# Computing the value rows of two contexts inside the router's closing steps, and moving key rotations and a root in the attention prelude

## The chip, the cores and the metric

The kernel is one program on one core of a Trainium2 chip. The metric is the device time of one execution in microseconds (us). A kernel's time is the median of several executions. A profile is one more execution, recorded by the hardware profiler; its times are counted from the start of its span.

The engines have short names in the profile: PE is TensorE (matrix multiplies), PEld is its load of the stationary operand, DVE is VectorE, ACT is ScalarE, POOL is GpSimd, and SP is the engine whose queue issues most of the transfers (SPq). Each engine works through its own instructions in order and waits on semaphores for the others.

## What is computed

The reference is a two-layer decoder in float32 with a layer norm after each residual:

```
x   [4, 512, 256]      ctx [4, 1601, 256]      out [4, 512, 256]
x = LN(x + ttt(x))                              # one inner gradient step per token
x = LN(x + softmax(q k^T / 16 + side) ctx)      # cross-attention, additive side mask [512, 1601]
x = LN(x + moe(x))                              # 8 experts of width 1024, the best 2 per token
x = LN(x + causal_self_attention(x, 16 heads))
x = LN(x + cross_attention(x, ctx, 16 heads))   # rotary positions on q and k, padding mask
x = LN(x + ffn(x))                              # integer weights, scaled back
```

Two parts matter here. The first is the router of the experts: `softmax(x Wr + br)`, the two best experts of each token, and for each token its rank among the tokens that chose the same expert, which is the row that it is copied to. The second is the input of the last cross-attention, which depends on the four contexts alone: keys `rope(ctx Wk + bk)` and values `ctx Wv`, for 1601 positions and 16 heads of 16 columns. The rotation multiplies by a cosine, the neighbour-swapped copy by a sine, and adds the two. The values do not depend on anything that the first layer computes.

## The kernel before

The kernel is one long function. Its stages, by the profile's clock, are:

- 0 to about 270 us: the first layer's inner-step part.
- To about 520: the first cross-attention and the router (pool `p2`, line 605 on). A loop goes over 4 contexts x 4 query tiles of 128 rows. Each step scores a tile against 1601 positions, transposes the exponentials, and multiplies them with the context (`weighted`). The contexts stand in SBUF transposed (`ctxTs[b]`) and in rows (`ctxa`, `ctxb`); the side mask is the tile `fs`.
- 523 to 1023: the experts, 23 blocks of 256 rows (8 fixed and 15 chosen at run time).
- 1024 to 1078: the prelude of the second layer's attention.
- To about 1480: self-attention, 16 units (4 sequences x 4 groups of four heads).
- To 2313: cross-attention, 16 more units, numbered 16 to 31.
- To 2438: the feed-forward part.

**The router's closing steps.** After the fourth query tile of a context, `closing(b)` is queued. It is a generator, and each call of `tail()` runs it to its next `yield`: statistics and the root of the variance; the four tiles normalised (line 726); nothing; the transposes of `to_xT` (lines 188 and 196); nothing; the logits of `route`; softmax; the first choice; the second choice; the counts (lines 485 to 497); the matmul of the ranks, `bank<-both,before`; and the target rows. For the first three contexts these steps are interleaved with the next context's work. For the last one nothing is left to interleave, so they run one behind the other. Then `scatter(3)` copies the rows of x to the buffer `xs` by eight indirect transfers on POOL (line 534), and `blocks_left()` works out which blocks the experts have to run. The PSUM buffers of `bank()` rotate over two.

The order of the instructions on every engine in this stage is the program's order (`tc.manual_schedule()`) up to `ordered.close()`; the few steps behind it are placed by a scheduler.

**The prelude.** `context(b, keys, values, here)` returns work items. A key item is a matmul, an eviction with bias by ACT into a tile `raw` (four buffers, shared with the rows of self-attention), a neighbour swap on DVE and three elementwise steps (`rotated`, lines 1149 to 1152), and a transfer of the result to DRAM (`kcd`) that SP issues one key item later. A value item is two matmuls of 128 positions and an ACT copy into `vals[b % 2]` (line 1191). Context 0's keys (`keys0`, eight items: two halves of four chunks, 512, 512, 512 and 65 positions wide) and the values of contexts 0 and 1 are done here. Beside them, `combined(0)` gathers the experts' outputs for sequence 0 and adds them (`add` holds the sums, the statistics, the root and the normalisation, lines 125 to 171), and `turn` transposes the result. `first_sums` does the same sums for sequence 1 on POOL, in four rounds (lines 1075, 1099 and 1100). `k0_` and `q0_` (line 1124) make the first rows of self-attention, which go through DRAM (`ksd`, `qd`) and come back regrouped by head.

**The units.** Each unit loops over tiles k of 128 keys. A step takes scores (line 1310), exponentials (line 1324) and the weighted sum of the step before (line 1337), and at the same time the next unit's scores are taken once more for their maxima (lines 202, 1267 and 1269). A list of work items per unit (`extras`) is spread over its steps. A step without an item does the weighted sum in two halves of 256 queries. A step with an item does it in one, followed by the item. In the kernel before, the keys and values of contexts 2 and 3 are such items, of the units 16 to 27:

```
later = [
    context(2, range(4), ()) + context(3, range(2), ()),
    context(3, range(2, 4), ()) + context(2, (), range(4)),
    context(3, (), range(4)),
]
```

Their source, `cx`, is loaded from the transposed context in chunks, two ahead. Unit 20 + n, for n from 0 to 7, holds 1, 4, 4, 4, 4, 3, 3 and 3 value items, 26 in all.

Of the kernel before, what the change touches and what calls it, by code (L numbers as in the profile page):

```python
# [9 lines left out]
F32 = mybir.dt.float32  # L10
# [7 lines left out]
P = 128  # L18
B, S, D = 4, 512, 256
S2 = 1601  # L20
NT = S // P
NKT = (S2 + P - 1) // P
# [3 lines left out]
NH, HD = 16, 16  # L26
# [8 lines left out]
def kn_of(kt):  # L35
    return P if kt < NKT - 1 else KLAST
# [3 lines left out]
def decoder(ctx: ExitStack, tc: tile.TileContext, a: dict, out: bass.AP):  # L40
    nc = tc.nc
# [16 lines left out]
    def bank():  # L58
        return psum["B"].tile([P, 512], F32, tag="bank", name="bank")
# [15 lines left out]
    def weight(pool, name):  # L75

        src = a[name]
        t = pool.tile([P, 2, src.shape[1]], F32, tag=name, name=name)
        nc.sync.dma_start(t, src.rearrange("(c p) n -> p c n", p=P))
        return t  # L80
# [117 lines left out]
    def mm(ps, terms):  # L198

        n = len(terms)  # L200
        for i, (l, r) in enumerate(terms):
            nc.tensor.matmul(ps, l, r, start=(i == 0), stop=(i == n - 1))  # L202
# [3 lines left out]
    p2in = ph2in.enter_context(tc.tile_pool(name="p2in", bufs=1))  # L206


    with (
# [15 lines left out]
        ps = wide()  # L225
# [4 lines left out]
        ps = bank()  # L230
# [7 lines left out]
        fs = p2in.tile([P, NT, S2], F32, tag="fs", name="fs")  # L238
# [7 lines left out]
        KHALF = (NKT + 1) // 2  # L246
# [121 lines left out]
        going, waiting, turn = [ttt(0)], [1, 2, 3], 0  # L368
# [236 lines left out]
        return wrow, xrow  # L605


    with tc.tile_pool(name="p2", bufs=2) as p2, ExitStack() as ordered:


# [5 lines left out]
        ps = wide()  # L616
# [3 lines left out]
        ps = bank()  # L620
# [3 lines left out]
        ps = wide()  # L624
# [3 lines left out]
        ps = bank()  # L628
# [7 lines left out]
        ctxTs, ctxns = {0: ctx_first[0]}, {0: ctx_first[1]}  # L636
# [105 lines left out]
        scored(*steps[0])  # L742
        tails = []

        def tail():
            if tails and next(tails[0], tails) is tails:
                tails.pop(0)

        for i in range(len(steps) + 1):
            if i + 1 < len(steps):  # L750
                b, t = steps[i + 1]
# [9 lines left out]
            if i > 0:  # L761
                b, t = steps[i - 1]
# [3 lines left out]
                        ctxns[b + 1] = load_ctx(b + 1)  # L766
                    tails.append(closing(b))
            tail()
        while tails:
            tail()  # L770
        ordered.close()
        scatter(B - 1, lambda inst: unordered("xs", inst))
        wrow, xrow = blocks_left()
    ph2in.close()


# [2 lines left out]


    QS = 1.0 / math.sqrt(HD)
    VW = HD + 1
    p4a = late_a.enter_context(tc.tile_pool(name="p4a", bufs=1))
    mrow = tc.dram_tile((4 * B, S2), F32, name="mrow")
    live = p4a.tile([P, 4 * B], F32, tag="live", name="live")
# [35 lines left out]
    with tc.tile_pool(name="p3", bufs=2) as p3, ExitStack() as ordered:  # L821
# [180 lines left out]
        n = E + NDYN  # L1002
# [23 lines left out]
    with ExitStack() as s4:  # L1026
# [17 lines left out]
        def one():  # L1044
            return spare() if alone else ps1.tile([P, 512], F32, tag="one", name="one")

        diagq, later_, qt, kself, ngs, vself, vals = (
            ready[k] for k in ("diagq", "later", "qt", "ks", "ngs", "vself", "vals")
        )
# [10 lines left out]
        index = {u: i for i, u in enumerate(units)}  # L1060
        extras = [[] for _ in range(len(units) + 3)]
        quiet = [[] for _ in range(len(units) + 3)]
        starts = [[] for _ in range(len(units) + 3)]
# [109 lines left out]
        def context(b, keys, values, here=None):  # L1173


            def key(src, i, c, eng):
                flush(1)
                k0, kw = chunks[i]
                ps = one()
                mm(ps[:, :kw], [(W["xaK"][:, h, c * P : (c + 1) * P], src()[h][:, :kw]) for h in range(2)])  # L1180
                raw = raw_tile()
                nc.scalar.activation(raw[:, :kw], ps[:, :kw], AF.Identity, bias=bkc[:, c : c + 1])  # L1182
                rotated(raw, kw, slice(k0, k0 + kw), eng, ready["turn", i] if here else None)
                going.append(lambda: to_rows(kcd[b], c, k0, kw, raw[:, :kw]))

            def value(src, k):
                kn, c0 = kn_of(k), (k % 4) * P
                ps = one()[:, :D]
                mm(ps[:kn], [(src()[c][:, c0 : c0 + kn], W["xaV"][:, c, :]) for c in range(2)])
                dst = vals[b % 2][:kn, k, : NH * VW].rearrange("p (h r) -> p h r", r=VW)  # L1190
                nc.scalar.copy(dst[:, :, :HD], ps[:kn].rearrange("p (h r) -> p h r", r=HD))

            items = []
            for i in sorted({*keys, *values}):
                if here is None:
                    src = lambda n=len(stream): chunk(n)
                    stream.append((b, i))
                else:
                    src = lambda i=i: here[2 * i : 2 * i + 2]
                eng = nc.gpsimd if here is None else nc.vector  # L1200
                if i in keys:
                    items += [lambda s=src, i=i, c=c: key(s, i, c, eng) for c in range(2)]
                if i in values:
                    items += [lambda s=src, k=k: value(s, k) for k in range(4 * i, min(4 * i + 4, NKT))]
            return items
# [339 lines left out]
        ends1, n = {}, 0  # L1545
# [55 lines left out]
        keys0 = context(0, range(4), (), here=qt + kself)  # L1601
        (k0_, q0_), rows0 = self_rows(0, 0)
        (k1_, q1_), rows1 = self_rows(0, 1)
        for f in keys0[0:2] + values1 + add + keys0[4:6] + turn:
            f()
        for f in (k0_, q0_, rows0, *self_values(0), *keys0[2:4], *keys0[6:8]):
            f()
# [2 lines left out]
        flush(0)  # L1610
        for i, (n0, n1) in enumerate(((0, 4), (4, 6), (6, 7), (7, 8))):
            extras[i] = ([k1_, q1_, rows1] if i == 0 else []) + keys1[n0:n1] + extras[i]
        later = [
            context(2, range(4), ()) + context(3, range(2), ()),
            context(3, range(2, 4), ()) + context(2, (), range(4)),
            context(3, (), range(4)),
        ]
        for b, work in enumerate(later):
            for g in range(NG):
                n = -(-len(work) // (NG - g))  # L1620
# [233 lines left out]
```

## Time and profile before

| | |
|---|---|
| median of 3 executions | 2437.68 us (2436.15 to 2438.79) |
| profiled execution | 2439.88 us |
| its span | 2438.0 us, 1.88 less |
| TensorE busy | 2344.4 us of the span (96%) |
| VectorE, ScalarE, GpSimd busy | 1211.7, 1073.5 and 422.7 us |
| TensorE busy in the stage 1480 to 2313 | 832.48 of 833 us |
| TensorE busy in the prelude, 1024 to 1078 | 47.40 of 54 us |

The page gives the busy time of each engine, then the span in 40 slices of 61 us, where the row PEclk is the clock that TensorE was granted, in tenths of full speed. The chain that ended last follows the last instruction back to whatever released it. A line of the timeline has the start, the duration (of a run of like instructions, if it ends in x2 or more), the engine, the source line, the operation with its tiles, the shapes, and in brackets how long the engine had been idle and what ended that. A line of the windows has the window and its length, then for each engine its busy time and its count of instructions, then the granted clock, the share of the transfer engines' time and the rate in GB/s.

### The profile page before, as it was taken

The page shows a single profiled execution, that of the slowest core. Times are in us where ns is not written, and L with a number is a line of the kernel's source. Part 1 is how long each engine was busy: PE and PEld are TensorE (multiplying, and loading weights), DVE is VectorE, ACT ScalarE, POOL GpSimd, SP SyncE. Part 2 cuts the span into 40 slices and gives each one's busy share as a digit, 9 for nine tenths or more (in the row PEclk, how much of TensorE's full clock was granted, in tenths as well). Part 3 has the DMA queues.
Part 4 walks back from the last instruction along what each step waited for, and adds up shares of the span by engine and source line. Part 5 has one row for each costly group of instructions (what it writes and reads, how often), then busy time and mean ns, then how long its engine had stood idle before and what let it go on. Part 6 is the DMA issues. An engine that isn't in the chain of part 4 may idle for free.

```text
span 2438.0 us, 34867 instructions
## 1 busy us (share of the span) xinstructions
PE 2344.4 (96%) x13928; PEld 1328.2 (54%) x13928; DVE 1211.7 (50%) x2854; ACT 1073.5 (44%) x1996; POOL 422.7 (17%) x429
## 2 busy tenths in 40 slices
PE   7898999959999999989999999999999999999998
PEld 4767677748888888843333334333333333333256
DVE  1333334322222233266656667666666666677334
ACT  1111122114444544424555453655666566566730
POOL 1010001121144433345130010222110010000000
PEclk9999999969999999989999997999999999999999
DMA  8300311145667555351211210112110110100100
GB/s 307 150 1 3 124 54 45 49 143 186 247 239 266 198 204 201 124 164 50 66 48 35 95 36 5 39 51 60 51 37 16 45 36 16 30 34 18 31 9 26
DMA packets 76112, 215.84 MB, mean 89 GB/s; under 512 B 11816, under 2 KB 35630, under 8 KB 66862
## 3 DMA queue, kind: packets, MB, share of 16 engines
q1 hardware_dynamic: 61790, 133.04, 16.1%
q0 software_dynamic: 10992, 65.54, 7.3%
q10 hardware_dynamic: 3168, 15.03, 1.8%
q8 instruction: 110, 1.80, 0.3%
q14 instruction: 52, 0.43, 0.1%
HBM read 171.53 MB, written 53.21 MB: 92 GB/s over the span
## 4 chain that ended last, share of the span: by engine, by line
PE 51%; ACT 1%; DVE 1%; issue 0%; DVEq 0%; ACTq 0%
PE s L1310 23%; PE one L202 12%; PE po L1337 11%; PE s L202 2%; PE s L1320 1%; PE one L1295 1%; PE one L1358 1%; ACT x L171 0%; ACT ex L1324 0%; DVE one L1269 0%; PE one L1379 0%; PE one L1477 0%; PE one L1400 0%; DVE pm L1267 0%; DVE st L156 0%
## 5 line engine op out<-in xcount | busy, mean ns | idle before, releaser
L1324 ACT ACTIVATE ex<-s 128x512 f32<-128x512 f32 (+1 forms) x1062 | 577.9, 594 | 466.9 <-PE s L1310 236.7
L1267 DVE TENSOR_REDUCE pm<-one 128x1 f32<-128x512 f32 x768 | 493.7, 685 | 174.5 <-PE s L1310 123.3
L1310 PE MATMUL s<-q,kc 32*128 32x512 f32 x1612 | 524.1, 640 | 0.2 <-ACT ex L1324 0.2
L202 PE MATMUL one<-kc,qt 32*128 32x512 f32 (+1 forms) x2048 | 483.8, 564 | 0.3 <-DVE pm L1267 0.3
L1310 PEld LDWEIGHTS s<-q,kc 32*128 32x128 f32 x1612 | 161.6, 179 | 210.9 <-issue 175.5
L1337 PE MATMUL po<-ex,v 128*32 128x256 f32 (+3 forms) x2472 | 245.1, 465 | 0.3 <-ACT ot L1350 0.3
L1269 DVE CUSTOM_DVE_ANT_0 one<-one,c_diagq 128x512 f32<-128x512 f32 x256 | 171.9, 716 | 75.6 <-PE one L202 63.5
L1310 PE MATMUL s<-q,ks 32*128 32x512 f32 x512 | 179.8, 650 | 5.3 <-ACT ex L1324 4.9
L1337 PEld LDWEIGHTS po<-ex,v 128*32 128x32 f32 (+1 forms) x2472 | 49.8, 108 | 232.2 <-issue 225.5
L886 DVE TENSOR_TENSOR g<-g,sg 128x1024 f32<-128x1024 f32 x46 | 57.2, 1243 | 235.8 <-ACT sg L883 235.7
L202 PE MATMUL wide<-xbT,eWi 128*128 128x256 f32 x736 | 168.9, 389 | 4.0 <-DVE xbT L858 4.0
L202 PEld LDWEIGHTS one<-kc,qt 32*128 32x128 f32 x2048 | 164.2, 188 | 11.6 <-DVE pm L1267 7.9
L202 PE MATMUL wide<-xbT,eWg 128*128 128x256 f32 x736 | 162.6, 379 | 0.0
L202 PE MATMUL bank<-eWo,g 128*128 128x256 f32 x736 | 162.5, 379 | 0.0
L202 PEld LDWEIGHTS wide<-xbT,eWi 128*128 128x128 f32 x736 | 143.5, 196 | 25.8 <-issue 4.2
L202 PE MATMUL one<-ks,qt 32*128 32x512 f32 x512 | 152.6, 665 | 3.7 <-ACT raw L1182 2.7
L202 PEld LDWEIGHTS wide<-xbT,eWg 128*128 128x128 f32 x736 | 139.7, 190 | 19.2 <-ACT g L883 0.2
L1150 POOL TENSOR_TENSOR raw<-raw,c_cos 128x512 f32<-128x512 f32 (+1 forms) x32 | 34.9, 1092 | 660.5 <-DVE swp L1149 578.1
L202 PEld LDWEIGHTS bank<-eWo,g 128*128 128x128 f32 x736 | 138.2, 190 | 17.9
L883 ACT ACTIVATE g<-wide,eWi 128x256 f32<-128x256 f32 x184 | 71.7, 476 | 72.3 <-PE wide L202 69.7
L1310 PEld LDWEIGHTS s<-q,ks 32*128 32x128 f32 x512 | 53.8, 185 | 83.4 <-issue 62.0
L202 PE MATMUL wide<-ctxT,q 128*128 128x512 f32 (+1 forms) x256 | 91.3, 510 | 0.8 <-DVE q L649 0.8
(319 smaller groups left out, 2988.4 us busy)
## 6 DMA issues: line engine op xcount, KB each, us to landing
xs<-zero SPq DMA_DIRECT2D x32, 512.0 KB
kc<-kcd SPq DMA_DIRECT2D x16, 800.5 KB
eWo<-in_eWo SPq DMA_DIRECT2D x8, 1408.0 KB
cx<-in_ctxT SPq DMA_DIRECT2D x18, 512.0 KB
eWi<-in_eWi SPq DMA_DIRECT2D x8, 1028.0 KB
eWg<-in_eWg SPq DMA_DIRECT2D x8, 1028.0 KB
qt<-qd SPq DMA_DIRECT2D x32, 256.0 KB
ctxT<-in_ctxT SPq DMA_DIRECT2D x4, 1601.0 KB
```

The costliest lines, as they stand in the source:

```text
L202: nc.tensor.matmul(ps, l, r, start=(i == 0), stop=(i == n - 1))
L883: nc.scalar.activation(dst[:, k, :], pv[:, k, :], func, bias=bias)
L886: nc.vector.tensor_tensor(part, part, dst, ALU.mult)
L1150: eng.tensor_tensor(raw[:, :n], raw[:, :n], cos[:, :n], ALU.mult)
L1267: nc.vector.tensor_reduce(pm[:, t, j, c : c + 1], ps, AX.X, ALU.max)
L1269: nc.vector.tensor_tensor_reduce(out=ps, in0=ps, in1=diagq[:, 384 - t * P : 896 - t * P], scale=1.0, scalar=LOWEST, op0=ALU.add, op1=ALU.m ...
L1295: nc.tensor.transpose(pt[:, t * P : (t + 1) * P], ng.rearrange("p j r -> p (j r)"), ident)
L1310: nc.tensor.matmul(ps[:kn], kt[rows, k * P : k * P + kn], q2[rows, :], start=True, stop=cross)
L1320: nc.tensor.matmul(ps[:, k * P : (k + 1) * P], later_[:, :P], later_[:, P:], start=False, stop=True)
L1324: nc.scalar.activation(ex[:kn, h, :], ps[:kn], AF.Exp)
L1337: nc.tensor.matmul(state["po"][j * 32 : j * 32 + 32, q0:q1], (vals if cross else vself)[b % 2][:kn, k, c0 : c0 + 32], ex[:kn, j % 2, q0:q1 ...
L1358: nc.tensor.transpose(pt[:, t * P : (t + 1) * P], ot[:, t * P : (t + 1) * P], ident)
```

## The change

The change has four parts.

1. The values of contexts 2 and 3 are computed in the router stage, from the contexts that stand there. They go into two tiles that take over the memory of the side mask and of half of the last context's rows. DVE sets the ones and zeros around them (six memsets, placed behind the second closing step). The 26 value steps stand between the closing steps of the last context: four ahead of the transposes, twelve ahead of the rank matmul, ten behind `blocks_left()`, which now comes before `ordered.close()` and `scatter(3)`. Three transfers write the values to DRAM (`vd`).
2. The cross units lose their 26 value items, and the lists become the keys of context 2 and the keys of context 3. One transfer per context loads the values at the start of an earlier unit.
3. In the prelude, `add`, with the root in it, stands between the eighth and the ninth value item of context 1, and `turn` comes before `keys0[4:6]`.
4. `eng`, the engine of the three rotation steps, is GpSimd for odd chunks of context 0's keys.

```diff
+    VW = HD + 1
+    VROW = NH * VW + HD - 1
+    vd = {b: tc.dram_tile((P, NKT * VROW), F32, name=f"vd{b}") for b in (2, 3)}
...
+        xaV = weight(p2, "xaV")
+        values, places = [], {}
+
+        def rows_of_values():
+            big = p2in.tile([P, NT * S2], F32, tag="fs", name="v23")
+            rest = p2in.tile([P, KHALF * D], F32, tag="ctxa", name="v2")
+            for i in range(NKT):
+                places[3, i] = big[:, i * VROW : (i + 1) * VROW]
+                j = NKT + i
+                places[2, i] = (
+                    big[:, j * VROW : (j + 1) * VROW] if i < 9 else rest[:, (i - 9) * VROW : (i - 8) * VROW]
+                )
+            for b_ in (2, 3):
+                nc.vector.memset(places[b_, NKT - 1], 0.0)
+            for t in (big[:, : 22 * VROW], rest[:, : 4 * VROW]):
+                t = t.rearrange("p (k r) -> p k r", r=VROW)
+                nc.vector.memset(t[:, :, NH * VW :], 0.0)
+                heads = t[:, :, : NH * VW].rearrange("p k (h r) -> p k h r", r=VW)
+                nc.vector.memset(heads[:, :, :, HD : HD + 1], 1.0)
+
+        def value(b, k):
+            kn = kn_of(k)
+            ps = bank()[:, :D]
+            mm(ps[:kn], [(ctxTs[b][:, c, k * P : k * P + kn], xaV[:, c, :]) for c in range(2)])
+            dst = places[b, k][:kn, : NH * VW].rearrange("p (h r) -> p h r", r=VW)
+            nc.scalar.copy(dst[:, :, :HD], ps[:kn].rearrange("p (h r) -> p h r", r=HD))
+            if b == 2 and k == NKT - 1:
+                nc.sync.dma_start(vd[2][:, : 9 * VROW], big_of(2, 0, 9))
+                nc.sync.dma_start(vd[2][:, 9 * VROW :], big_of(2, 9, NKT))
+            if b == 3 and k == NKT - 1:
+                nc.sync.dma_start(vd[3], big_of(3, 0, NKT))
...
-        while tails:
-            tail()
+        values = [lambda b=b, k=k: value(b, k) for b in (2, 3) for k in range(NKT)]
+        for n in (0, 4, 0, 0, 0, 12, 0, 0, 0, 0, 0):
+            if n == 4:
+                tail()
+                rows_of_values()
+            else:
+                tail()
+            for f in values[:n]:
+                f()
+            values = values[n:]
+        wrow, xrow = blocks_left()
+        for f in values:
+            f()
         ordered.close()
         scatter(B - 1, lambda inst: unordered("xs", inst))
-        wrow, xrow = blocks_left()
...
-                eng = nc.gpsimd if here is None else nc.vector
+                eng = nc.gpsimd if here is None or i % 2 else nc.vector
                 if i in keys:
                     items += [lambda s=src, i=i, c=c: key(s, i, c, eng) for c in range(2)]
...
-        for f in keys0[0:2] + values1 + add + keys0[4:6] + turn:
+        for f in keys0[0:2] + values1[:8] + add + values1[8:] + turn + keys0[4:6]:
             f()
         for f in (k0_, q0_, rows0, *self_values(0), *keys0[2:4], *keys0[6:8]):
             f()
...
-        later = [
-            context(2, range(4), ()) + context(3, range(2), ()),
-            context(3, range(2, 4), ()) + context(2, (), range(4)),
-            context(3, (), range(4)),
-        ]
+        later = [context(2, range(4), ()), context(3, range(4), ())]
+        for b in (2, 3):
+            starts[index[b - 1, 1, True]].append(
+                lambda b=b: nc.sync.dma_start(vals[b % 2].rearrange("p k r -> p (k r)"), vd[b])
+            )
```

More of the change, by code (lines that the diff above doesn't have):

```diff
@@ L743, in decoder, with big_of @@
         tails = []
+        xaV = weight(p2, "xaV")
[27 more added lines that the diff above has]
+                nc.sync.dma_start(vd[3], big_of(3, 0, NKT))
+        def big_of(b, k0, k1):
+            first = places[b, k0]
+            return bass.AP(first.tensor, first.offset, [first.ap[0], [1, (k1 - k0) * VROW]])
         def tail():
@@ L768, in decoder @@
             tail()
-        while tails:
-            tail()
+        values = [lambda b=b, k=k: value(b, k) for b in (2, 3) for k in range(NKT)]
[8 more added lines that the diff above has]
+            values = values[n:]
+        assert not tails
+        wrow, xrow = blocks_left()
+        for f in values:
+            f()
         ordered.close()
         scatter(B - 1, lambda inst: unordered("xs", inst))
-        wrow, xrow = blocks_left()
     ph2in.close()
@@ L781, in decoder @@
     QS = 1.0 / math.sqrt(HD)
-    VW = HD + 1
     p4a = late_a.enter_context(tc.tile_pool(name="p4a", bufs=1))
```

## The prediction

> **What bounds the kernel now.** I read the page first, then the windows by stage, then the timeline of the three places that the change touches. All times are us from the start of the span.
>
> ```profile
> PE 2344.4 (96%) x13928; PEld 1328.2 (54%) x13928; DVE 1211.7 (50%) x2854; ACT 1073.5 (44%) x1996; POOL 422.7 (17%) x429
> PEclk9999999969999999989999997999999999999999
> PE 51%; ACT 1%; DVE 1%; issue 0%; DVEq 0%; ACTq 0%
> ...
> 1054.00:1073.00 19.00, 17.52 (x65) 10.15 (x63) 9.30 (x18) 9.37 (x20) 12.18 (x12) 1.00 0.55 165
> 1073.00:1097.00 24.00, 21.27 (x50) 7.10 (x48) 16.05 (x52) 2.51 (x5) 1.48 (x2) 0.65 0.64 200
> 1700.00:2190.00 490.00, 489.80 (x3819) 174.45 (x3818) 335.34 (x617) 294.54 (x560) 36.12 (x30) 1.00 0.11 35
> ```
>
> The first three lines are the page (busy time by engine, granted clock by slice, chain that ended last); the rest are windows, with the busy time of PE, PEld, DVE, ACT and POOL, then clock and DMA. TensorE is the bound, and in 1700 to 2190, inside the cross units, it has 0.2 idle: there an instruction taken off PE is time gained in full. In the ninth slice (the router, 488 to 549) and around 1080 (the prelude's end, the window's 0.65) the clock is down, and PE waits on a chain of other engines: there a delay of the chain is time lost. The change does one of each.
>
> **Part 1: the router's tail (loss).** The timeline shows the last context's closing:
>
> ```profile
> 490.37 2.30 PE L188 MATMUL wide<-ident,x 128*128 128x128 f32 x8 [3.19 <-DVE x L726]
> 499.78 0.19 DVE L466 COPY lg<-bank 128x32 f32<-128x32 f32 x1 [8.49 <-PE bank L202]
> 505.49 0.64 PE L202 MATMUL bank<-both,before 128*128 128x32 f32 x2 [5.75 <-DVE both L492]
> 508.79 0.96 POOL L534 DMA_INDIRECT xs<-x,rows  x1 [1.15 <-DVE cum L562]
> 522.99 1.09 PE L854 MATMUL bank<-ident,xb 128*128 128x128 f32 x4 [15.80 <-DMA xb<-xs]
> ```
>
> Everything to 522.99 is one chain: transposes, logits, softmax and top two on DVE (499.78 to 505.49, 5.7), ranks, eight scatters of 1.26 each, the reload of xb, the first expert. TensorE runs in program order, so a value placed ahead of a link delays it.
> - Four values stand before the transposes. The third needs a bank that ACT empties, ACT's copy writes a tile that DVE's six memsets fill, and these stand behind DVE's apply, which ends at 491.28. The two 128x287 and the strided ones hold 1.5 thousand elements a row: at 0.69 for 512 elements (DVE's rotation row) with six starts I estimate 1.6, so copies begin near 492.9. Two copies (0.37), two values (0.86 to 1.13 each by the value rows of the prelude and of the cross units): the transposes end near 496 instead of 492.7, and to 497.8 if the values run at half clock. The logits took 5.97 here, cold, and 3.4 at 461.24 when warm. So the logits are ready at 500.8 (warm) to 502.6, against 499.74.
> - Twelve values stand before the rank matmul. At 0.86 (ACT-paced copies 0.37 + 0.49 in the prelude) they take 10.3, to 12.1 partly cold, and cover the DVE chain of 5.7: 4.6 to 6.4 more.
> - The ranks now come ahead of the matmul and DVE steps that count blocks, −0.5.
>
> First scatter 513.7 to 517.2 instead of 508.79: I take **+7** (4.5 to 9). The last ten values (8.6) lie beside the eight scatters (10.1): nothing, though if the scatters began early they'd cost up to 2 on the first transposes. After them PE idles some 7 again, so the first expert still starts cold (32 matmuls in 10.09, the next 32 in 7.07): no gain. The three stores of 1.32, 0.59 and 1.91 MB stand on SP ahead of later loads; SP reaches qkvQ, which needs the last store landed, some 25 later than at 487, but those weights are read from 1024 on and the expert weights behind them from 560 on, at least 40 later: nothing, up to +2 in the range.
>
> The Trainium skill, "TensorE: Matmul & The Clock Gate", Part 1, says that sustained activity over one window of about 3.4 us lifts the clock to full; by that the values would keep PE warm through the logits, and this part would be +4.9 (an estimate, the low end with the warm logits row). The row speaks against relying on it: the clock was at half in 490 to 531 and again in a 3.4 stretch at 466 right behind small matmuls, though PE was occupied.
>
> **Part 2: the prelude (loss).** Here the change moves rotations from DVE to GpSimd. The edit reads "odd chunks on GpSimd", four rotations. But the lambdas take `eng` when they run, after the loop, and the last chunk is odd: the instruction order of the changed kernel has all **eight** rotations' 24 tensor_tensors on POOL, behind the four rounds of sums for context 1 that POOL runs first.
>
> ```profile
> 1059.44 0.69 DVE L1150 TENSOR_TENSOR raw<-raw,xT 128x512 f32<-128x512 f32 x1
> 1062.37 1.99 POOL L1099 TENSOR_SCALAR y<-y,ws 128x256 f32<-128x256 f32 x1
> 1063.48 0.60 ACT L1124 ACTIVATE raw<-one 128x512 f32<-128x512 f32 x1 [1.12 <-PE one L202]
> 1078.20 0.69 DVE L1269 CUSTOM_DVE_ANT_0 one<-one,c_diagq 128x512 f32<-128x512 f32 x1
> 1097.43 1.27 POOL L1150 TENSOR_TENSOR raw<-raw,c_cos 128x512 f32<-128x512 f32 x1 [22.87 <-DMA cx<-in_ctxT]
> ```
>
> The rows: a rotation step on DVE 0.69 and on POOL 1.27 (three take 3.85); a step of the sums beside DVE's rotations 1.99, alone 0.92; the query's eviction; the first maximum of the first attention unit. In before the first rotation begins on DVE at 1037.99. On POOL it waits for the sums. Their rounds start at 1041.17 and took 6.6 each while undisturbed, 10 and 9 beside DVE's rotations, ending at 1074.56. With these gone I put their end at 1069.5 (1068 if all four are undisturbed, 1073 if little changes). Call it P0.
> - The raw tiles are a ring of four. The query's eviction is the sixth user, and its slot is free only when the second rotated key has been written to DRAM: P0 + 2 x 3.85 + 0.6 to issue + 4.1 to land (ksd issued 1062.38, read 1066.46) = P0 + 12.4, say P0 + 12, against 1063.48. ACT, and behind it PE, stand in order: the four self values, the later keys and the first scores all queue behind this eviction.
> - From the eviction to the first maximum took 14.7 before (qd written and read 4.8, then further keys, rotations and their stores); without DVE's last small rotation step I take 14.0. POOL's own work to its last rotation ends about P0 + 25.
>
> So the first maximum is at P0 + 26 = 1095.5 instead of 1078.20: **+17** (P0 from 1068 to 1073 gives +16 to +21; down to +14 if the stores land faster). Nothing gives it back behind: in 1097 to 1130 PE is busy 32.6 of 33. DVE sheds 18 x 0.69 + 6 x 0.23 = 13.8 of work, but no DVE work bounds the stage after that. The root between values[7] and [8] lets ACT apply and turn earlier than 1055.24 by a few us; since the query's eviction waits for the slot, it is worth nothing, at most −1.
>
> The Trainium skill, "GPSIMD Engine Reference", section 3.1, puts a GpSimd tensor_tensor at 1.96 times VectorE's, which speaks against this move; the rows give 1.84. By the page a step would be an estimated 1.35, the two rotations on the path 0.5 longer; no part of the sum uses it.
>
> **Part 3: the cross units (gain).**
>
> ```profile
> 1995.89 0.64 PE L1337 MATMUL po<-ex,v 128*32 128x256 f32 x8
> 1997.74 1.06 PE L1337 MATMUL po<-ex,v 128*32 128x512 f32 x8
> 1999.81 1.13 PE L202 MATMUL one<-xaV,cx 128*128 128x256 f32 x4
> 2001.94 0.64 PE L1337 MATMUL po<-ex,v 128*32 128x256 f32 x8
> ```
>
> A step of the loop over keys: without an item two halves of weighting (0.64), with a value one whole (1.06) and the value's four matmuls (1.13). By the starts of these matmuls, a filled step is 2001.94 − 1997.74 = 4.20, which is also the median of the 24 steps with a value; the 88 plain ones have median 3.49. The 26 values of contexts 2 and 3 leave eight units: 26 x (4.20 − 3.49) = **−18.5**. By means (4.31 and 3.72) it is −15.3, by the value's own 0.92 to 1.06 of PE −24 to −27.6. The values come back as one load of 1.91 MB per context, issued a unit or more before its use, over 100 earlier, at a DMA share of 0.11: nothing; without that cover a load would be 6 or more (1.91 MB at the first slice's 307 GB/s).
>
> **Sum.** +7 + 17 − 18.5 = +5.5. The profiled execution was 2439.88 (span 2438.0 and 1.88 around it), 2.20 over the median of 2437.68. So 2445.4 for such an execution, **2443.2** against the median.
>
> **Rivals.**
> - (a) No change: the three terms cancel nearer. Sums end at 1068 and the stores land fast (+14), router +5: +0.5, 2438. For it: P0 is an extrapolation; against: two of the three must be low.
> - (b) Faster: the prelude's wait is hidden. One mechanism: the query's eviction is not held by the ring (a slot released when the rotation reads it, or the first two rotations before the sums). It decides when the eviction comes before about 1069, which leaves Part 2 at 0: 7 − 18.5 = −11.5, 2426. For it: only 4 rotations would be expected from the edit. Against: the instruction order shows the wait and all eight behind the sums.
> - (c) Worse: sums still stretched by DVE's accumulations (P0 = 1073, +21), logits and twelve values cold (+9), values worth their means (−15.3): +14.7, 2452.
>
> **How the numbers follow.** A measurement of this kernel tells about 0.2%, 4.9 us, from none. My forecast (all three terms as told) 0.55, (a) 0.15, (b) 0.15, (c) 0.15. Of the forecast's 0.55, its terms' bounds leave about 0.35 above +4.9 and 0.2 within. So slower 0.35 + 0.15 = 0.50, the same 0.2 + 0.12 = 0.32, faster 0.15 + 0.03 = 0.18. The range leaves out most of (b) and the far end of (c): from −7 to +16, 2431 to 2454.
>
> **What would show it.** Right: first scatter near 515; no POOL rotation before about 1068 and the query's eviction near 1081; first maximum near 1095; the units 20 to 27 shorter by 0.7 a value, no xaV matmul after 1490. Wrong: rotations between the sums or on DVE, an eviction before 1070, plain steps longer than 3.49 once the values have gone, or a clock that stays full through the router and takes the first expert from 10.1 to 7.1 (−3).

## The result, and the profile after

The changed kernel takes 2444.36 us (median of 20 executions, 2433.2 to 2450.45), the kernel before 2436.47 us (median of 20, 2431.0 to 2444.49). The ratio is 1.003 with a 95% interval of 1.0021 to 1.0039: slower by 7.9 us (5 to 9.5 by the interval). The prediction was 2443.2, with 2431 to 2454 as its range and "slower" as the likeliest case. One execution of the kernel before, beside the runs from the root order to the placed version with the bound engine, took 9464.62 us; it is left out of all ratios and medians here.

The profiled execution took 2446.97, with a span of 2445.2, 7.2 longer than the span before. Both profiled executions lie above their medians, by 2.6 and 3.4. The page and a window answer to the lines of before:

```profile
PE 2351.0 (96%) x14144; PEld 1337.1 (55%) x14144; DVE 1200.2 (49%) x2836; ACT 1075.0 (44%) x1996; POOL 444.6 (18%) x453
PEclk9999999989999999988999998999999999999999
...
1062.00:1083.00 21.00, 8.84 (x27) 4.46 (x25) 0.91 (x4) 2.29 (x4) 18.16 (x19) 0.77 0.20 61
1700.00:2190.00 490.00, 489.43 (x4026) 172.40 (x4026) 343.75 (x637) 293.83 (x548) 51.61 (x44) 1.00 0.12 40
```

DVE lost 11.5 of work and POOL gained 21.9. The cross units are still TensorE's (489.43 of 490). The new thing is the window 1062 to 1083: TensorE works for 8.84 of 21, DVE for 0.91, ACT for 2.29, and only POOL, with 18.16, for most of the time.

I cut each profiled execution at the same seven places. A row is a distance between two events, so a different start of the first stage, which varied by 5 between executions, drops out of all rows but the first.

| stretch (us) | before | after | difference | predicted |
|---|---|---|---|---|
| start to the end of the last weighted matmul of the first cross-attention | 487.19 | 486.94 | −0.25 | 0 |
| from there to the first expert's transposes | 35.80 | 47.33 | +11.5 | +7 |
| experts, to the first matmul of the prelude | 501.01 | 497.42 | −3.6 | 0 |
| prelude, to the first maximum of unit 0 | 54.20 | 70.88 | +16.7 | +17 |
| from there to the end of unit 0 | 51.41 | 48.31 | −3.1 | 0 |
| units 1 to 15 | 358.16 | 359.41 | +1.3 | 0 |
| cross units 16 to 31 | 826.09 | 810.92 | −15.2 | −18.5 |
| feed-forward part | 124.15 | 123.98 | −0.2 | 0 |

**The router after.** The same events as in the fence of before, in the timeline of the changed kernel, with two rows for the values:

```profile
492.93 0.65 ACT L776 COPY v<-bank 128x256 f32<-128x256 f32 x2 [3.31 <-DVE v L769]
493.35 3.44 PE L202 MATMUL bank<-xaV,ctxT 128*128 128x256 f32 x8 [4.68 <-ACT v L776]
503.98 13.57 PE L202 MATMUL bank<-xaV,ctxT 128*128 128x256 f32 x48
504.08 0.19 DVE L466 COPY lg<-bank 128x32 f32<-128x32 f32 x1 [11.08 <-PE bank L202]
517.38 0.30 PE L202 MATMUL bank<-both,before 128*128 128x32 f32 x2
519.57 0.96 POOL L534 DMA_INDIRECT xs<-x,rows  x1 [16.13 <-DVE n L544]
534.27 1.09 PE L908 MATMUL bank<-ident,xb 128*128 128x128 f32 x4 [6.06 <-DMA xb<-xs]
```

The second row is the wait that the prediction worked out: TensorE stands still for 4.68 before the third value, because ACT's copy (first row) waited for DVE's memsets. The third row is the twelve values: 13.57 in one block, while DVE's chain behind the logits (504.08) needs 5.3 to the counts. The rank matmul stands behind that block at 517.38.

**The prelude after.**

```profile
1075.17 1.26 POOL L1204 TENSOR_TENSOR raw<-raw,xT 128x512 f32<-128x512 f32 x1
1083.24 0.60 ACT L1178 ACTIVATE raw<-one 128x512 f32<-128x512 f32 x1 [16.84 <-DMA kcd<-raw]
1086.92 0.60 ACT L1178 ACTIVATE raw<-one 128x512 f32<-128x512 f32 x1 [3.09 <-DMA kcd<-raw]
1102.44 0.01 DVE L1203 LOAD_MASK_SELECT swp<-raw  x1 [3.19 <-POOL raw L1206]
1102.57 0.69 DVE L1323 CUSTOM_DVE_ANT_0 one<-one,c_diagq 128x512 f32<-128x512 f32 x1
```

The first rotation begins on POOL at 1075.17, right behind the last sum. ACT, idle for 16.84 and then 3.09, waits for the two transfers of rotated keys before it may evict the first self-attention rows; the third row is the query's eviction, 11.75 behind the first rotation. The last two rows show what holds the first maximum: a neighbour swap ahead of it on DVE that waits for POOL to release one of the two `swp` buffers.

### The profile page after: what moved, and what is told of

Same layout as the page of the kernel before. It is cut to its first block, busy times and chain, and to the rows that moved or that the text cites. A ratio compares the mean times of both kernels' runs of the same rounds, so it can differ in the third digit from the quotient of the medians.

```text
span 2445.2 us, 35304 instructions
## 1 busy us (share of the span) xinstructions
PE 2351.0 (96%) x14144; PEld 1337.1 (55%) x14144; DVE 1200.2 (49%) x2836; ACT 1075.0 (44%) x1996; POOL 444.6 (18%) x453
## 4 chain that ended last, share of the span: by engine, by line
PE 50%; DVE 1%; ACT 1%; issue 0%; DVEq 0%; ACTq 0%
PE s L1364 22%; PE po L1391 11%; PE one L202 11%; PE s L202 2%; PE s L1374 1%; PE one L1349 1%; PE one L1412 1%; ACT x L171 0%; ACT ex L1378 0%; DVE pm L1321 0%; DVE one L1323 0%; PE one L1433 0%; PE one L1531 0%; PE one L1454 0%; DVE nb L166 0%
## 5 line engine op out<-in xcount | busy, mean ns | idle before, releaser
L1364 PE MATMUL s<-q,kc 32*128 32x512 f32 x1612 | 530.9, 641 | 0.8 <-ACT ex L1378 0.8
L1364 PEld LDWEIGHTS s<-q,kc 32*128 32x128 f32 x1612 | 166.5, 179 | 204.6 <-issue 172.1
L1391 PE MATMUL po<-ex,v 128*32 128x256 f32 (+3 forms) x2688 | 252.2, 444 | 0.3 <-ACT ot L1404 0.3
```

What stands on the lines that cost most here:

```text
L1364: nc.tensor.matmul(ps[:kn], kt[rows, k * P : k * P + kn], q2[rows, :], start=True, stop=cross)
L1391: nc.tensor.matmul(state["po"][j * 32 : j * 32 + 32, q0:q1], (vals if cross else vself)[b % 2][:kn, k, c0 : c0 + 32], ex[:kn, j % 2, q0:q1 ...
```

## The experiments

Each run was taken with its own executions of the kernel before. Ratios are to those, with their 95% intervals.

### The engine bound per chunk

```diff
-                    items += [lambda s=src, i=i, c=c: key(s, i, c, eng) for c in range(2)]
+                    items += [lambda s=src, i=i, c=c, eng=eng: key(s, i, c, eng) for c in range(2)]
```

> The changed kernel, with the engine bound per chunk, so that chunks 0 and 2 of the keys rotate on DVE again and only chunks 1 and 3 on POOL. Theory (the eviction of the first query waits for the second rotated key's raw tile, and that rotation waits for the sums on POOL): the query's eviction is back near 1071 instead of 1086.92, POOL's four rotations lie behind the sums, the first maximum comes near 1090 instead of 1102.57, and the time falls by 9 to 13 against the changed kernel, to about 2433. Rival (the cost is GpSimd's slower step, 24 x 0.58 = 14, wherever it stands): half of the rotations remain, so only about half of the loss goes, 6 to 7, to about 2438.

Measured: 2427.5, ratio 0.9959 (0.9943 to 0.9975): 9.1 faster than before, and some 17 faster than the changed kernel. The timeline of this run:

```profile
1070.21 0.60 ACT L1178 ACTIVATE raw<-one 128x512 f32<-128x512 f32 x1 [1.12 <-PE one L202]
1080.10 1.27 POOL L1204 TENSOR_TENSOR raw<-raw,xT 128x512 f32<-128x512 f32 x1
1087.88 0.69 DVE L1323 CUSTOM_DVE_ANT_0 one<-one,c_diagq 128x512 f32<-128x512 f32 x1
```

The query's eviction is back at 1070.21 and waits for TensorE, not for a transfer. POOL's first rotation is even later than in the changed kernel (1080.10, since the sums run beside DVE again), and yet the first maximum comes 14.7 earlier. Prelude: 55.98, against 54.20 before and 70.88 after. Moving half of the rotations back took away nearly all of the loss, so the rival that counts GpSimd's slower steps falls. The gain over the changed kernel, some 17, was larger than the 9 to 13 that I expected; 14.9 of it is the prelude.

### The values part alone

The edit undoes parts 3 and 4 of the change.

```diff
-                eng = nc.gpsimd if here is None or i % 2 else nc.vector
+                eng = nc.gpsimd if here is None else nc.vector
...
-        for f in keys0[0:2] + values1[:8] + add + values1[8:] + turn + keys0[4:6]:
+        for f in keys0[0:2] + values1 + add + keys0[4:6] + turn:
```

> The values part alone: router, stores, loads and cross units as in the changed kernel, the prelude with its order and its DVE rotations as before. Theory (the terms add): the first expert starts 11.3 later than before, the experts give back 3.6 by the clock, the cross units 15.2; the first maximum lies 7.7 later than in the kernel before; in sum -7.5, about 2429. Rival (the prelude's shift and the cross units' gain hang together, the gain being a matter of how the units fall): less than 10 gained in the cross units, the time 2434 or more.

Measured: 2427.95, ratio 0.9963 (0.9949 to 0.9976), 8.7 faster than before. The router costs 47.16, the experts 498.24, the prelude 53.12, the cross units 811.19. In these rows the terms add (about 2429 was expected), and the cross units' gain does not hang on the prelude.

### The prelude part alone

The edit is parts 3 and 4 of the change on the kernel before.

> The prelude part alone, on the kernel before: the root between the values and the rotations as the changed kernel has them, the values of contexts 2 and 3 still in the cross units. Theory: the first maximum 16 to 17 later than 1078.20, 3 of it given back in unit 0 by the clock, so +13 to +17, about 2450 to 2453. Rival (the prelude costs little by itself and the changed kernel loses its time in the router): +5 or less.

Measured: 2448.3, ratio 1.0053 (1.0035 to 1.0071), 11.7 slower. That is a little under the 13 to 17 expected, and far above the rival's 5. The prelude took 69.99, 15.8 more than before, by the same chain: the rotation begins at 1063.31 behind the sums, the query's eviction follows at 1075.06.

### All eight rotations on GpSimd, the sums behind them

```diff
         for f in fetch:
             f()
-        for f in first_sums:
-            f()
...
         for f in (k0_, q0_, rows0, *self_values(0), *keys0[2:4], *keys0[6:8]):
             f()
+        for f in first_sums:
+            f()
```

> The changed kernel with all eight rotations on POOL, but the four rounds of sums for sequence 1 issued behind the prelude's keys instead of ahead of them. Theory (the wait behind the sums is what costs, not the engine): rotations start near 1047, the query's eviction is back near 1071, the first maximum near 1087 instead of 1102.57; 10 to 14 less than the changed kernel, about 2431 to 2434. Rival (GpSimd's rate: 24 steps at 0.58 more each): at most 3 less than the changed kernel, 2441 or more. A third outcome: the sums come too late for unit 1 and take the place of the wait, then unit 1 shows it.

Measured: 2441.64, ratio 1.0011 (0.9999 to 1.0024), against 2444.36 for the changed kernel: 2.7 less, not the theory's 10 to 14. By the time alone the rival, GpSimd's rate (at most 3 less, 2441 or more), is the one that is met. The timeline and the windows of unit 0 tell them apart:

```profile
1048.86 1.28 POOL L1204 TENSOR_TENSOR raw<-raw,xT 128x512 f32<-128x512 f32 x1
1074.23 0.60 ACT L1178 ACTIVATE raw<-one 128x512 f32<-128x512 f32 x1 [1.12 <-PE one L202]
1088.81 0.69 DVE L1323 CUSTOM_DVE_ANT_0 one<-one,c_diagq 128x512 f32<-128x512 f32 x1
...
1123.03 1.27 POOL L1204 TENSOR_TENSOR raw<-raw,c_cos 128x512 f32<-128x512 f32 x1
...
1089.00:1110.00 21.00, 21.00 (x51) 6.79 (x49) 13.20 (x43) 1.88 (x3) 11.98 (x18) 0.70 0.68 220
1110.00:1146.00 36.00, 34.34 (x164) 11.65 (x162) 21.82 (x72) 13.99 (x27) 25.42 (x24) 0.81 0.21 55
```

The prelude behaves as told: rotations from 1048.86, the eviction without a wait on a transfer, the first maximum at 1088.81, 13.8 earlier than in the changed kernel. It takes 56.75, close to the 55.98 of the run with the bound engine. So the wait behind the sums is what costs in the prelude, although all 24 steps run on GpSimd. But unit 0 gave much of it back: 57.53 from the first maximum to the unit's end, against 45.8 to 51.4 in the other runs. There the sums stand on POOL until 1123.07, and the first rotation of context 1's keys only follows (last row of the timeline; 1097.43 before). The third outcome, sums too late for unit 1, is not what this shows: units 1 to 15 took 355.07, less than in any other run. In unit 0 TensorE was idle for just 1.7, in 1110 to 1146, and its granted clock was 0.70 up to 1110 and 0.81 behind; why its clock was lower there stays open.

### The root order alone

The edit is part 3 of the change on the kernel before, all rotations on DVE.

> The kernel before with the root order alone: add stands between the eighth and the ninth value item and turn ahead of keys0[4:6]; all rotations on DVE, the values in the cross units. Theory (the root was not on the path): within 1 of the kernel before, 2435.5 to 2437.5. Rival (the eviction of the first query comes earlier by what the root gains, some 3): 2433.

Measured: 2439.78, ratio 1.0018 (1.0006 to 1.0031): no gain, and a loss of some 4 (1.5 to 7.5 by the interval), more than the 1 that I allowed. The timeline of this run shows why there is no gain:

```profile
1045.72 0.30 ACT L125 ACTIVATE sd<-mv,eps 128x4 f32<-128x4 f32 x1 [3.60 <-DVE mv L161]
1050.63 1.73 PE L1105 MATMUL one<-ident,x 128*128 128x128 f32 x8
1059.27 0.60 ACT L1124 ACTIVATE raw<-one 128x512 f32<-128x512 f32 x1 [1.12 <-PE one L202]
```

Counted from the first matmul of the prelude (1019.90 here, 1024.00 before), the root comes at 25.8 instead of 31.2, the transposes at 30.7 instead of 34.2, but the query's eviction at 39.4 instead of 39.5: the two key matmuls that stood ahead of the transposes now stand behind them. The prelude took 55.68 with this order, and 55.98 and 55.64 in the runs with the bound engine; with the old order it took 50.2 to 54.2 in six runs. Against 54.20 before, the prelude accounts for some 1.5 of the loss; the rest was not traced, and the run with the bound engine, which has this order too, does not show it in its time (2427.5 against 2427.95 without).

### The values placed in TensorE's idle stretches

On the values part alone. The large tile's memsets go ahead of the last weighted matmul, and the 26 values are dealt out as 3 behind that matmul, 3 behind the softmax and 20 behind the counting of the blocks. (`rows_of_big` and `rows_of_rest` are the two halves of `rows_of_values`.)

```diff
                 b, t = steps[i - 1]
+                if i == len(steps):
+                    rows_of_big()
                 weighted(b, t)
...
-        for n in (0, 4, 0, 0, 0, 12, 0, 0, 0, 0, 0):
-            if n == 4:
-                tail()
-                rows_of_values()
-            else:
-                tail()
-            for f in values[:n]:
-                f()
-            values = values[n:]
+        some(3)
+        for i, n in enumerate((0, 0, 0, 0, 0, 3, 0, 0, 0, 0, 0)):
+            tail()
+            if i == 0:
+                rows_of_rest()
+            some(n)
```

> The values part with the prelude of before, but placed by the idle stretches of PE: the large tile's memsets run before the last weighted matmul, three values stand right behind that matmul, three behind the softmax, the other twenty behind the counting of the blocks, beside the scatters. Theory (a value ahead of a link of the chain costs, beside it not): the logits reach DVE at 499 to 501 instead of 504.56 in the run with the values part alone, the rank matmul stands at 506 instead of 517.91, the first scatter at 509 to 510, the first expert's transposes at 523 to 527 instead of 534.58; 7 to 11 less than that run, about 2418 to 2422. Rival (the stores on SP ahead of the first expert's load, or the colder clock, take it back): 2426 or more.

Measured: 2419.19, ratio 0.9936 (0.9914 to 0.9958), 14.1 faster than before by the medians. In this execution the last weighted matmul ended at 482.14, 5 earlier than in the run with the values part alone, so the rows are to be read as distances:

```profile
491.94 0.19 DVE L466 COPY lg<-bank 128x32 f32<-128x32 f32 x1 [4.89 <-PE bank L202]
498.93 18.99 PE L202 MATMUL bank<-xaV,ctxT 128*128 128x256 f32 x80
500.27 0.96 POOL L534 DMA_INDIRECT xs<-x,rows  x1 [3.89 <-DVE n L544]
517.95 0.37 SPq L897 DMA_DIRECT2D xb<-xs  x1
521.04 0.63 PE L916 MATMUL bank<-ident,xb 128*128 128x128 f32 x4 [3.12 <-DMA xb<-xs]
```

| from the end of the last weighted matmul | before | values alone | placed | all behind | memsets early | twelve behind |
|---|---|---|---|---|---|---|
| to the softmax's first step | 12.59 | 17.15 | 9.80 | 12.81 | 11.12 | 17.14 |
| from there to the rank matmul | 5.71 | 13.35 | 5.67 | 5.58 | 12.99 | 5.67 |
| from there to the first scatter | 3.30 | 2.18 | 2.66 | 2.99 | 2.19 | 2.89 |
| all, to the first expert's transposes | 35.80 | 47.16 | 38.91 | 47.45 | 40.90 | 50.57 |

The distance to the first expert is 8.25 shorter than with the values part alone. The softmax comes even earlier than in the kernel before (9.80 against 12.59): the three values fill the stretch in which DVE takes the statistics, and the eight transposes take 1.16 where they took 2.30 before, the logits 3.5 where they took 5.97. What is left is the twenty values (18.99): SP issues the first expert's load (517.95) only when the last of them is done, 8.7 behind the last scatter, where 2.5 lay between the two before.

The time shows less than the rows. The interval of this run overlaps that of the values part alone (0.9949 to 0.9976), and the run that follows, whose router is 8.5 longer, is only 2.5 slower by the medians. So the shorter router is shown in the profiles; how much of it reaches the time is not settled.

### All 26 values behind

The same, with none ahead: `some(0)` and eleven zeros.

> As the placed version, but all 26 values behind the counting of the blocks, none ahead. Theory: the chain up to the first scatter is that of the kernel before, 508.8 or 0.5 earlier, and 26 values of 0.86 to 1.7 end at 530 to 534, so the first expert starts 7 to 11 later than 522.99; about 2427, no better than the values part alone. Rival (warm throughout and only the last store counts): first expert at 526, 2422.

Measured: 2421.67, ratio 0.9946 (0.9927 to 0.9965). The chain up to the first scatter is that of before (column "all behind"), and the values take 24.26 behind it; the first expert starts 47.45 after the last weighted matmul, as late as with the values part alone. By the rows that is the theory's end. The time is not: the theory said about 2427, and 2421.67 is the rival's number (2422), without its first expert at 526 (529.58 here, in an execution whose first stage was 5 shorter, too). Why the time came out better than the rows was not found.

### The placed version with the bound engine

The placement above, with the root order and the four rotations of the bound engine.

> The placed version with the changed prelude and the engine bound per chunk (four rotations on POOL, the root between the values). Theory: that prelude was worth within 1 of the old one (2427.5 against 2427.95 with the values as changed), so the same as the placed version within 2, about 2418 to 2422.

Measured: 2418.44, ratio 0.9933 (0.9915 to 0.995), 14.8 faster than before by the medians. It beats both kernels, as the placed one does (2419.19); the two are not told apart.

### The memsets early, the values where the change has them

As placed, but with 4 values and 12 where the change has them (10 behind).

> The values part alone with its values where the change has them (4, 12, 10), but the large tile's memsets ahead of the last weighted matmul instead of behind DVE's normalisation. Theory (the third value waits for a bank, the bank for an ACT copy, the copy for the memsets): TensorE has no gap of 4.7 between the second and the third value, the transposes stand some 5 earlier, and from the end of the last weighted matmul to the softmax's first step there are 12 to 13 instead of 17.4; the twelve values cost what they did (13.4 from there to the rank matmul). Rival (the four values themselves cost it): the distance stays above 16.

Measured: 2418.18, beside 2433.16 for the kernel before on the same chip, one execution each, so the rows are what counts. The timeline:

```profile
484.94 1.99 PE L202 MATMUL bank<-xaV,ctxT 128*128 128x256 f32 x8 [1.27 <-ACT v L780]
493.06 0.19 DVE L466 COPY lg<-bank 128x32 f32<-128x32 f32 x1 [6.20 <-PE bank L202]
506.05 0.30 PE L202 MATMUL bank<-both,before 128*128 128x32 f32 x2
```

The gap before the third value is 1.27 instead of 4.68, and the softmax comes 11.12 after the last weighted matmul instead of 17.15. That is 6.0 less, and a little below the 12 to 13 expected, because the logits are warmer as well (4.1 instead of 5.3). The twelve values cost what they did, 12.99. So the first four cost nothing by themselves; the memsets behind DVE's normalisation did.

### The twelve values behind, the memsets late

On the values part alone.

```diff
-        for n in (0, 4, 0, 0, 0, 12, 0, 0, 0, 0, 0):
+        for n in (0, 4, 0, 0, 0, 0, 0, 0, 0, 0, 0):
```

> The values part alone with its first four values and late memsets, but the twelve values behind the counting of the blocks with the ten. Theory: the distance from the softmax's first step to the rank matmul falls from 13.4 to the 5.7 of DVE's chain, the first scatter comes 7 to 8 earlier than in the run with the values part alone, but 22 values then stand behind it (19 to 22), so that the first expert starts only 1 to 4 earlier. Rival (the twelve are hidden by the DVE chain but for 5): the first scatter 5 earlier at most.

Measured: 2431.58, beside 2433.16 for the kernel before, one execution each. The distance from the softmax to the rank matmul is DVE's chain again (5.67), and the first scatter comes 7 earlier, as told. But the first expert came 3.4 later, not 1 to 4 earlier:

```profile
512.53 0.96 POOL L534 DMA_INDIRECT xs<-x,rows  x1 [9.24 <-DVE n L544]
523.55 10.63 PE L202 MATMUL bank<-xaV,ctxT 128*128 128x256 f32 x48 [0.21 <-issue]
537.41 1.09 PE L908 MATMUL bank<-ident,xb 128*128 128x128 f32 x4 [3.23 <-DMA xb<-xs]
```

The scatters are over by 522.5, but the 22 values run to 534.2, and the load behind them, which SP issues at 534.21, lands at 537.4. With all 26 behind, too, SP issues that load (526.44) when the last value is done (526.41). The clock was at half from 499.6 to 516.7, over the first of them. So the ten values behind the scatters are hidden, as the prediction had it; twenty are not.

## Why the prediction was right

The sign and the mechanisms of the three parts hold: +5.5 was predicted, +7.2 is the difference of the spans, +7.9 that of the medians. That the sum came so close is partly luck, since two of its terms were off and two stages outside it made up for them. Point by point:

- **Part 2, +17: right, by its own chain.** The first maximum came 16.7 later in the prelude. The three links are in the fence: P0 at 1075.17 is 43.5 after the prelude's first matmul (predicted 45.5: all four rounds of sums ran undisturbed, 26.5 in all instead of 33.4); the query's eviction follows 11.75 later (predicted 12); the first maximum follows 27.4 after P0 (predicted 26). The bound engine removed the loss with half of the rotations still on POOL, the later sums removed it from the prelude with all of them there: it is the wait behind the sums, passed on by the ring of four tiles, and not the engine's rate. Of the 16.7, 14.9 goes with the eight rotations behind the sums; the other 1.8 is there with the bound engine, too, and with the new order alone (1.5). One link was not named. I had the first maximum follow the query's eviction through its rows and the further keys; in the profile its last releaser is the ring of two `swp` buffers, which POOL multiplies and releases and DVE waits for in order. ACT had evicted the key of that last swap at 1099.99 (1099.67 and 0.32), 2.4 before the swap, so the path that I named ends close by, and the number held. A larger ring, which would test this by itself, was not tried.
- **Part 1, +7: the mechanism right, the size too small; 11.5.** Two terms were mis-sized. The logits, told for 500.8 to 502.6, were ready at 504.08: the four values, memset wait included, cost 4.55 and not 1.1 to 2.9. The copies did begin at 492.9 as estimated, but the clock was at half in 492.9 to 496.3 and again from 499.7, so that the last two values took 3.44 and the logits 5.3. And the twelve values, told for 10.3 to 12.1, took 13.3 from the softmax's first step to the rank matmul, since the clock stayed at half to 509.9; that term is 7.6 instead of 4.6 to 6.4. The counting behind the ranks gave 1.1 (told for 0.5), and the ten values beside the scatters cost 0.5 at most (14.70 from the first scatter to the first expert, 14.20 before). The experts, at 497.42, show no wait for the stores and weights that queue behind.
- **Part 3, −18.5: right; −15.2 in the table.** Of the missing 3.3, 3.2 is a stretch of half clock in units 28 and 29 (104.20 for the two, 101.02 before), which the profiled execution of before did not have. The run with the root order alone has the values in the cross units and that stretch; its cross units took 828.21, and like against like the values are worth 828.21 − 810.92 = 17.3, or 0.66 each. Against the profile of before, without units 28 and 29, it is 18.3, or 0.71 each, which is what I took. The sign that I gave, units 20 to 27 shorter by 0.7 a value, shows only in units 24 to 27, which lose 13 values and nothing else: 9.8 shorter, 0.76 each. Units 20 to 23 also take over four key items from units 16 to 19; they are 0.9 shorter, and units 16 to 19 are 7.6 shorter.
- **Experts and unit 0, −3.6 and −3.1: not in the prediction, and not of the change.** The run with the root order alone has the old router, and its experts took 498.31, too; unit 0 took between 45.8 and 51.4 in the runs but one. The profile of before had a long stretch of half clock that reached 7.8 into the experts (489.8 to 530.8), and another of 6.8 in them. In unit 0 the length goes with the mean granted clock: 45.78, 48.31, 51.41 and 57.53 at 0.90 (bound engine), 0.85 (changed kernel), 0.81 (before) and 0.77 (later sums). Part 1 (4.5 too low) and Part 3 (3.3 too much gain) erred to the same side, and these 6.7 took it back in the difference of the spans: the sum was closer than its terms. How the medians' 7.9 divides among the parts is not settled to better than some 5: the values part alone (−8.7) and the prelude part alone (+11.7) add to +3.0, and the intervals of the three runs (about 3, 4 and 2 to each side) are wide enough for that.
- **The root, "worth nothing, at most −1": right that it gains nothing**, but the order alone cost some 4 (1.5 to 7.5), which the sum did not have.
- **The weighed rules.** The Trainium skill, "TensorE: Matmul & The Clock Gate", Part 1, made Part 1 +4.9, by my estimate, through a clock that the values keep up. Of my two rows against it only the one at 466 speaks: in 490 to 531 TensorE was busy for just 17.2 of 41. In the changed kernel that did not happen: TensorE was occupied for 10.00 of 10 in the window 500 to 510, at a clock of 0.50. In the placed version, where the gap of 4.68 is gone, the transposes and logits did run at the warm durations (1.16 and 3.5). So these runs show both, and the occupancy that the profile shows does not tell which. "GPSIMD Engine Reference", section 3.1, gives GpSimd 1.96 times VectorE's time; the rotation steps took 1.26 against 0.69, 1.83 times.
- **The faster rival, 2426, with four rotations instead of eight**, is close to what the run with the bound engine measured, 2427.5, 9.1 below its own runs of before where the rival had 11.5. Its mechanism was right: the eviction is not held, and the prelude costs 1.8 instead of 16.7. Its total came out by the same luck as the forecast's, as the router cost 11.4 there, too. What kept it from being the result is that the lambdas read `eng` after the loop.

## What to carry to other kernels

Read the instruction order for where moved work lands, not the edit: a variable that a deferred call reads late put twice the work on an engine, behind other work in that engine's queue, and its price was the wait through a ring of buffers and not the engine's rate. When work is moved into idle stretches of a chain, place it by which link it stands ahead of: a value behind the last matmul, with its buffers prepared early, made the chain shorter, while the same value waiting for memsets, or twelve ahead of a link that needed 5.7, made it longer. Compare stage by stage between fixed events and over several profiles, since a single profile's clock can move a stage by 3 without any cause found in the kernel.

## What the runs showed of the hardware

The granted clock was at half in stretches in which the profile shows TensorE busy without a gap. Three windows of the changed kernel, the first in the router, the others late in unit 28 and behind it:

```profile
500.00:510.00 10.00, 10.00 (x31) 8.69 (x32) 4.83 (x29) 1.35 (x4) 1.72 (x2) 0.50 0.08 27
...
2189.00:2193.00 4.00, 3.80 (x24) 0.99 (x18) 3.44 (x9) 3.81 (x8) 0.00 (x0) 0.97 0.00 0
2193.00:2197.00 4.00, 4.00 (x23) 0.92 (x24) 1.45 (x5) 1.97 (x4) 0.00 (x0) 0.50 0.00 0
```

In the last window TensorE is busy for 4.00 of 4, at a clock of 0.50. In the changed kernel this half clock lasted 6.83 and cost 3.2 over units 28 and 29. It stood at the same place in ten of the twelve profiled executions (6.83 in eight of them, 3.41 in two), with the values in the units or not, and in two (the kernel before and the prelude part alone) it was missing. What starts it was not settled.

In all twelve profiles every stretch of half clock that ended inside the span lasted 3.41 or a whole multiple of it. The one in the router, from 499.73 to 509.97, is three times 3.41. Up to 503.98 it holds the router's matmuls with 8 columns, then the twelve values (128x256); its last third, from 506.56, is the first that holds values alone, and the clock is full from its end. Whether the small matmuls are what kept the clock down was not tested.
